# Moving the output projection one unit later, and part of a convolution from VectorE to ScalarE and GpSimd, in a two-layer attention kernel

## The chip, the core and the metric

The kernel runs on one NeuronCore of a Trainium2 chip. A core has five engines with a queue of instructions each: TensorE (PE; its weight loads are shown apart, as PEld), VectorE (DVE), ScalarE (ACT), GpSimd (POOL) and SyncE (SP), which here only issues DMAs. The engines meet at semaphores. The metric is the device time of one execution in microseconds (us); the profile comes from one execution of its own.

## The reference, cut to what matters

Two layers follow each other on an input of 8 images with 32 x 32 positions and 512 channels, all in float32. The first layer is group norm and self-attention (8 heads of 64 over all 1024 positions). The second layer is attention whose keys and values are sampled at learned places:

```python
x_ln = layernorm(x); q = x_ln @ wq + bq
o = depthwise_conv7x7_stride2(q, dw_w)           # 1024 positions -> 256, 49 taps a channel
o = gelu(o + dw_b)
offsets = conv1x1(o, pw_w)                       # 512 channels -> 2
grid = refs + tanh(offsets)                      # 256 places in the image
interp = bilinear_sample(x, grid)                # 4 rows of x weighted, for each place
k = v = interp @ wv + bv
attn = softmax((q @ mq_w) (k @ mk_w)^T); att = attn @ (v @ mv_w)     # 8 heads, 1024 x 256
z = att @ mo_w + mo_b + x
out = gelu(layernorm(z) @ mlp_w + mlp_b) + z
```

Everything is computed, and in float32. The convolution, the sampling and what depends on them are per image; one convolution chunk is 128 channels of one image (4 chunks an image).

## The kernel before, in words

The kernel has two passes, one for each layer, with tensors in DRAM between them (`mid` is the first layer's result, `hat_d` its normalised transpose). The first pass also computes the convolution of images 0 to 5 (`EARLY = 6`); there ScalarE multiplies a tap into a buffer (`part_x`) and GpSimd adds it to the sum (`oa`), while VectorE does other taps in one instruction each (`od`). The convolution of images 6 and 7 (8 chunks) is left to the second pass, which is what the change touches.

The second pass runs 64 **units**. A unit is one pair of heads (`hp`, 4 of them) of one half of an image (`hi`, 16 of them: 512 queries against 256 keys), `n = 4*hi + hp`. Nothing is scheduled by a planner: each step is entered with `at(place, step)`, a place is a unit's number plus a fraction, `run_due` sorts all steps by place, and a wrapper (`InOrder`) keeps every engine's instructions in that program order. So the fractions are the order in every queue, SP's and POOL's too, and an instruction that waits holds up all that stands behind it on its engine.

What a unit `n` does before the change, in order of place:

- `n`: `scores` (PE: `sc`; DVE: two row maxima `nmax`; ACT: 8 exponentials `e`).
- `n + 0.09`, `0.1`: `product` of the unit before (PE: `av`, needs `et`), `scale` (DVE: `attH`).
- `n + 0.11`, `0.13`: `moved` for each head (DVE: block transpose `sq`; SP: `sq` to DRAM as `sq_d`, and back, re-ordered, as `et`).
- `n + 0.12`: `joined`, the output projection of one tile of 128 rows, of the half image whose four units came before (PE: `wo`; DVE: `z` and its statistics; POOL: one power, `mv`, for the norm). The power is written by `rstd`.
- `n + 0.17`: `query_step` for the next unit (PE: `hat_h`; ACT: `q`).
- `n + 0.26` to `0.93`: nine convolution taps on DVE (`chunk`), with `norm` (DVE: `zn`) at `0.47`, `fill` of the next convolution chunk (PE: `wq_r`; DVE: `pad`) at about `0.5`, `share` (DVE: `rep`) at `0.54`.
- `n + 0.6`, `0.62`, `0.72`: `turned` (PE transposes `zn`; ACT: `zT`), `turn` (PE transposes `rep`; ACT: `inv`), `mlp` (PE: `wm`).
- `n + 0.95` to `0.97`: `biased` (DVE: `res`), and for every second tile the GELU of two tiles (ACT, with a table load each way), and `end` (POOL: `res + z` and the DMA out, twice).

Rows of `x` for the residual (`xr`) are fetched for two tiles at once at `pair - 0.7` (SP) and get their bias at `pair - 0.5` (POOL), where `pair` is the first of the two tiles' places. Once an image, at places counted from `last = 8*b - 4`: `conv_gelu`, `offsets`, `targets` (17 small DVE instructions), two times `gather` (POOL: 4 indirect DMAs, `row`) and `sample` (DVE: 4 instructions, `smp`); then four `key_step` and two `value_step` on PE. The PSUM pool for projections has three buffers (`mm`), used in turn.

The queue order of the four places that matter for what follows can be read in `back_steps` (`places`), `unit_steps`, `conv_steps` and `point_steps`:

Of the kernel before, what the change touches and what calls it, by code (L numbers as in the profile page):

```python
# [17 lines left out]
P = 128  # L18
# [213 lines left out]
def attention_then_deformable_attention(  # L232
# [115 lines left out]
    def at(place, step):  # L348
        due.append((place, len(due), step))
# [452 lines left out]
    with ExitStack() as l1:  # L802
# [52 lines left out]
        pads = [cv.tile([P, PADH, PADW], F32, tag=f"pad{i}", name=f"pad{i}") for i in range(PADS)]  # L855
        for pad in pads:
            nc.gpsimd.memset(pad, 0.0)
        att = Attention(nc, ident, ps_mm, ps_sc, ps_av, work, dram)
        smps = {}

# [52 lines left out]
            hat = chat[b, cb]  # L913
            room["ps"] = project(lambda c: hat[:, par * NC + c, :], lambda c: wq_r[:, c, :])

        def fill_end(cb, par):
            conv_pad(pads[cb % PADS], room["ps"], bq_row, par)

        def tap(b, cb, i):
            if i == 0:  # L920
                room["chunk"] = cv.tile([P, NS], F32, tag="chunk", name="chunk", bufs=2)
            conv_tap(room["chunk"], pads[cb % PADS], dww, cb, i, i == 0)
            if i == KS * KS - 1:
                nc.gpsimd.dma_start(o_d[b][:, cb, :], room["chunk"])

        def conv_gelu(b):
            o = room[b, "o"]
# [3 lines left out]
        def offsets(b):  # L931
            o = room[b, "o"]
            ps = mm_tile()
            for h in range(2):
                for cb in range(NC):
                    nc.tensor.matmul(
                        ps[:, ts(h, 2)], lhsT=o[:, cb, ts(h, P)], rhs=pww[:, cb, :],
                        start=(cb == 0), stop=(cb == NC - 1),
                    )
            room["th"] = cv.tile([P, 4], F32, tag="th", name="th")  # L940
            nc.scalar.activation(room["th"], ps[:, 0:4], AF.Tanh)

        def targets(b):
            room[b, "ii"], room[b, "wt"] = corners(room["th"])
# [110 lines left out]
        def back_steps(hi, start, step, tail=False):  # L1055

            b, half = divmod(hi, 2)
            xs = mid[b].rearrange("(t p e) c -> e t p c", e=2, p=P)[half]
            outs = out_tok[b].rearrange("(t p e) c -> e t p c", e=2, p=P)[half]
            xr, z, zn, zT, res = {}, {}, {}, {}, {}  # L1060

            def fetch(t):
                xr[t] = tmp("xr", 4)
                nc.sync.dma_start(xr[t], xs[t])

            def add(t):
                nc.gpsimd.tensor_tensor(xr[t], xr[t], bo_row, ALU.add)

            def joined(t):
                ps = project(lambda c: attH[hi][:, c, ts(t, P)], lambda c: wo[:, c, :])  # L1070
                z[t] = tmp("z", 5)
                nc.vector.tensor_tensor(z[t], ps, xr[t], ALU.add)
                stats = work.tile([P, 6], F32, tag="stats", name="stats")
                mv = xr["mv", t] = work.tile([P, 3], F32, tag="mv", name="mv")
                nc.vector.bn_stats(stats, z[t])
                nc.vector.bn_aggr(mv[:, 0:2], stats)
                rstd(mv[:, 2:3], mv[:, 1:2], 1e-5)

            def norm(t):
                zn[t], mv = tmp("zn", 2), xr["mv", t]  # L1080
                nc.vector.tensor_scalar(
                    zn[t], z[t], mv[:, 0:1], mv[:, 2:3], ALU.subtract, ALU.mult
                )

            def turned(t):
                ps = mm_tile()
                for c in range(NC):
                    nc.tensor.transpose(ps[:, ts(c, P)], zn[t][:, ts(c, P)], ident)
                zT[t] = tmp("zT", 2)
                nc.scalar.copy(zT[t], ps)  # L1090

            def mlp(t):
                res["ps", t] = project(lambda c: zT[t][:, ts(c, P)], lambda c: wm[:, c, :])

            def biased(t):
                res[t] = tmp("res", 3)
                nc.vector.tensor_tensor(res[t], res["ps", t], bm_row, ALU.add)

            def gelu(t):
                nc.scalar.activation(res[t], res[t], AF.Gelu)  # L1100

            def end(t):
                nc.gpsimd.tensor_tensor(res[t], res[t], z[t], ALU.add)
                nc.gpsimd.dma_start(outs[t], res[t])

            for t in range(NC):
                n, pair = start + step * t, start + step * (t - t % 2)
                places = (pair - 0.7, pair - 0.5), (n + 0.12, n + 0.47), (n + 0.6, n + 0.72, n + 0.95)
                if tail:
                    places = (n - 0.7, n - 0.6), (n, n + 0.01), (n + 0.11, n + 0.12, n + 0.125)  # L1110
                steps = (fetch, add), (joined, norm), (turned, mlp, biased)
                for place, what in zip(sum(places, ()), sum(steps, ())):
                    at(place, lambda t=t, what=what: what(t))


                if t % 2 == 1:
                    for what, after in ((gelu, 0.96), (end, 0.97)):
                        for i in (t - 1, t):
                            at(n + (0.13 if tail else after), lambda i=i, what=what: what(i))

        def unit_steps(n):
            hi, hp = divmod(n, NHP)
            b = hi // 2
            u = dict(tiles=NQT, at=0, v=lambda j, h: vals[b][:, j, ds((2 * hp + h) * HD, HD)])

            def scores():
                u["q"], u["k"] = queries.pop((hi, hp)), keys[b][:, hp, :]
                u["e"] = att.scores(u)  # L1130

            def scale():
                if hp == 0:
                    attH[hi] = work.tile([P, NHP, QB], F32, tag="attH", name="attH")
                att.scale(attH[hi][:, hp, :])

            at(n, scores)
            at(n + 0.11, lambda: att.moved(u, 0))
            at(n + 0.13, lambda: att.moved(u, 1))
            at(n + 0.54, lambda: att.share(u["sums"]))  # L1140
            at(n + 0.62, att.turn)
            at(n + 1.09, lambda: att.product(u))
            at(n + 1.1, scale)
            if n + 1 < 2 * B * NHP:
                at(n + 0.17, lambda: query_step(*divmod(n + 1, NHP)))


        def conv_counts():
            taps = (B - EARLY) * NC * KS * KS
            return [0, 0] + [9] * (taps // 9) + [taps % 9]  # L1150

        def conv_places():

            places = []
            for n, count in enumerate(conv_counts()):
                for j in range(count):
                    x = j / count
                    x = 0.26 + 0.2 * x / 0.45 if x < 0.45 else 0.57 + 0.36 * (x - 0.45) / 0.55
                    places.append(n + x)
            taps = KS * KS  # L1160
            return [places[i : i + taps] for i in range(0, len(places), taps)]

        def conv_steps():
            chunks, filled = conv_places(), -2
            for k, places in enumerate(chunks):
                b, cb = EARLY + k // NC, k % NC
                free = max(filled, chunks[k - PADS][-1] if k >= PADS else filled)
                slots = [n + 0.49 for n in range(60) if free < n + 0.49 < places[0] - 0.05]
                slots = (slots[:2] if k < PADS else slots[-2:]) if len(slots) > 1 else [slots[0], slots[0] + 0.26]
                filled = slots[1]  # L1170
                at(slots[0] - 1.8, lambda b=b, cb=cb: conv_fetch(b, cb))
                for par, place in enumerate(slots):
                    at(place, lambda b=b, cb=cb, par=par: fill(b, cb, par))
                    at(place + 0.04, lambda cb=cb, par=par: fill_end(cb, par))
                for i, place in enumerate(places):
                    at(place, lambda b=b, cb=cb, i=i: tap(b, cb, i))

        def point_steps(b):
            last = 2 * NHP * b - NHP
# [1 line left out]
            at(last - 0.035, lambda: conv_gelu(b))  # L1181
            at(last + 0.535, lambda: offsets(b))
            at(last + 0.75, lambda: targets(b))
            for h, (p0, p1) in enumerate(((0.8, 1.3), (1.31, 1.7))):
                at(last + p0, lambda h=h: gather(b, h))
                at(last + p1, lambda h=h: sample(b, h))

            first = 2 * NHP * b
            for hp, place in enumerate((-1.82, -1.81, 0.48, 2.18)):
                at(max(first + place, last + 2.18), lambda hp=hp: key_step(b, hp))  # L1190
            for t, place in enumerate((-0.82, 0.11)):
                at(first + place, lambda t=t: value_step(b, t))

        def load_late():
# [32 lines left out]
        for hi in range(2 * B):  # L1227
            if hi > 1:
                at(NHP * (hi - 1) - 1, lambda hi=hi: fetch_hat(hi))
            if hi + 1 < 2 * B:  # L1230
                back_steps(hi, NHP * (hi + 1), 1)
            else:
                back_steps(hi, NHP * (hi + 1) + 0.2, 0.1, tail=True)
        run_due(float("inf"))


# [31 lines left out]
```

## Time and profile before

| | before |
|---|---|
| median of 3 runs | 3657.85 us (3655.79 to 3663.18) |
| the profiled execution | 3652.66 us, of which the span from the first to the last instruction is 3650.9 us |
| first pass and preparation of the second | 0 to 2307.8 us |
| units 0 to 62 of the second pass | 2307.8 to 3580.7 us |
| unit 63 and the end | 3580.7 to 3650.9 us |

A unit's start is the start of its first `sc` matmul. All instructions carry line 54, that of the wrapper, so groups are told apart by the tiles that they write and read. "Idle before" in a timeline is the time for which the engine stood still before the instruction, and behind the arrow stands what ended it. Busy times are recorded for a matmul from its start to a modelled end, so neighbours overlap by about 0.1 us. A matmul in float32 is recorded twice (4 matmuls are x8).

### The profile page before, as it was taken

The page shows a single profiled execution, that of the slowest core. Times are in us where ns is not written, and L with a number is a line of the kernel's source. Part 1 is how long each engine was busy: PE and PEld are TensorE (multiplying, and loading weights), DVE is VectorE, ACT ScalarE, POOL GpSimd, SP SyncE. Part 2 cuts the span into 40 slices and gives each one's busy share as a digit, 9 for nine tenths or more (in the row PEclk, how much of TensorE's full clock was granted, in tenths as well). Part 3 has the DMA queues.
Part 4 walks back from the last instruction along what each step waited for, and adds up shares of the span by engine and source line. Part 5 has one row for each costly group of instructions (what it writes and reads, how often), then busy time and mean ns, then how long its engine had stood idle before and what let it go on. Part 6 is the DMA issues. An engine that isn't in the chain of part 4 may idle for free. (4 is left out here: it accounts for less than half of the span.)

```text
span 3650.9 us, 45574 instructions
## 1 busy us (share of the span) xinstructions
PE 3477.3 (95%) x15128; PEld 1743.3 (48%) x15128; DVE 2585.2 (71%) x3614; ACT 1763.8 (48%) x3740; POOL 1382.4 (38%) x1667
## 2 busy tenths in 40 slices
PE   7999999999999999999999989889999998989997
PEld 4554554554554554554554544444444444444443
DVE  4767688888888888888887873376766766674553
ACT  3443365575575575575575541234333433344442
POOL 1002236646646646646646634022222222221312
PEclk9999999999999999999999999999999999999999
DMA  4656657657657657657656665344444444354442
GB/s 143 162 153 174 179 151 209 173 152 207 174 153 206 176 151 202 180 151 199 182 147 193 193 168 175 117 164 155 168 159 145 167 146 174 129 180 167 173 143 100
DMA packets 358268, 606.00 MB, mean 166 GB/s; under 512 B 54577, under 2 KB 152881, under 8 KB 355985
## 3 DMA queue, kind: packets, MB, share of 16 engines
q1 hardware_dynamic: 327072, 499.94, 46.0%
q0 software_dynamic: 29808, 101.05, 8.9%
q8 instruction: 121, 1.98, 0.2%
q10 hardware_dynamic: 1152, 2.10, 0.2%
q14 instruction: 115, 0.93, 0.1%
HBM read 212.83 MB, written 121.63 MB: 92 GB/s over the span
## 5 line engine op out<-in xcount | busy, mean ns | idle before, releaser
L54 ACT ACTIVATE e<-sc,nmax 128x1024 f32<-128x1024 f32 (+1 forms) x1024 | 803.7, 798 | 665.4 <-DVE nmax L54 664.8
L54 DVE TENSOR_REDUCE nmax<-sc 128x1 f32<-128x1024 f32 (+1 forms) x640 | 752.2, 1216 | 328.3 <-PE sc L54 327.3
L54 DVE STREAM_TRANSPOSE sq<-e 128x1024 f32<-128x1024 f32 x640 | 767.0, 1229 | 167.0 <-ACT e L54 148.8
L54 POOL TENSOR_TENSOR oa<-part_x,oa 128x256 f32<-128x256 f32 x852 | 646.7, 759 | 589.1 <-ACT part_x L54 543.4
L54 PE MATMUL sc<-k,q 64*128 64x512 f32 x2048 | 535.2, 619 | 15.4 <-ACT e L54 13.5
L54 ACT ACTIVATE part_x<-pad_x,dww_x 128x256 f32<-128x256 f32 x852 | 437.3, 543 | 231.4 <-POOL oa L54 228.9
L54 PE MATMUL av<-et,v 128*64 128x256 f32 x4096 | 501.3, 387 | 8.5 <-DMA et<-sq 7.9
L54 PE MATMUL mm<-xT,wqkv 128*128 128x512 f32 x1024 | 470.1, 603 | 3.1 <-issue 3.1
L54 PEld LDWEIGHTS av<-et,v 128*64 128x64 f32 x4096 | 274.1, 137 | 313.3 <-issue 162.1
L54 POOL TENSOR_TENSOR mv<-mv,minus_half 128x1 f32<-128x1 f32 x128 | 79.5, 621 | 764.7 <-DVE mv L54 758.2
L54 PEld LDWEIGHTS sc<-k,q 64*128 64x128 f32 x2048 | 185.8, 186 | 276.5 <-issue 193.3
L54 PEld LDWEIGHTS mm<-xT,wqkv 128*128 128x128 f32 x1024 | 187.6, 191 | 234.9 <-issue 229.2
L54 PE MATMUL mm<-wm,zT 128*128 128x512 f32 x512 | 265.2, 666 | 8.2 <-ACT zT L54 6.2
L54 PEld LDWEIGHTS mm<-wqkv,xT 128*128 128x128 f32 x2048 | 234.2, 192 | 20.4 <-issue 18.9
L54 PE MATMUL mm<-wqkv,xT 128*128 128x128 f32 x2048 | 243.4, 277 | 0.0
L54 PE MATMUL mm<-wo,attH 128*128 128x512 f32 x512 | 235.6, 603 | 0.0
L54 PE MATMUL mm<-w,attT 128*128 128x512 f32 x512 | 234.0, 602 | 0.0
L54 PE MATMUL mm<-hat_h,wqq 128*128 128x512 f32 x512 | 230.6, 593 | 0.0
L54 DVE SCALAR_TENSOR_TENSOR od<-pad_x,dww_x,od 128x256 f32<-128x256 f32 x276 | 218.4, 791 | 5.5
L54 ACT ACTIVATION_READ_ACCUMULATOR e<-sc,nmax 128x1 f32 x1024 | 209.1, 204 | 0.0
L54 POOL TENSOR_TENSOR xr<-xr,bo_row 128x512 f32<-128x512 f32 x64 | 82.1, 1301 | 332.4 <-DMA xr<-mid 229.7
L54 DVE SCALAR_TENSOR_TENSOR chunk<-pad,dww,chunk 128x256 f32<-128x256 f32 x384 | 190.9, 497 | 9.9
(159 smaller groups left out, 3621.5 us busy)
## 6 DMA issues: line engine op xcount, KB each, us to landing
et<-sq SPq DMA_DIRECT2D x2048, 128.0 KB, 2.7
sq_d<-sq SPq DMA_DIRECT2D x128, 512.0 KB, 2.8
et<-sq_d SPq DMA_DIRECT2D x128, 512.0 KB, 3.9
hat_h<-hat_d SPq DMA_DIRECT2D x16, 1024.0 KB, 7.1
xr<-mid SPq DMA_DIRECT2D x64, 256.0 KB, 4.3
out_dram<-res POOLq DMA_DIRECT2D x64, 256.0 KB, 2.3
x<-in_x_dram POOLq DMA_DIRECT2D x60, 256.0 KB, 3.9
w<-in_L_conv_w_out_dram POOLq DMA_DIRECT2D x14, 1024.0 KB, 7.7
```

What stands on the lines that cost most here:

```text
L54: return self.tc.keep_in_program_order(op(*args, **kwargs))
```

## The change

All edits are in the second pass.

1. `joined` moves from `n + 0.12` to `n + 0.05`, ahead of `product` (from `n + 0.09` to `n + 0.15`), and the whole back end of a half image (`back_steps`) starts one unit later, `NHP * (hi + 1) + 1`. `norm` moves from `n + 0.47` to `n + 0.13`, between the two `moved`. `share` moves from `0.54` to `0.2`. `end` and its pair of `fetch` and `add` keep their fractions, so they shift by one unit, from odd to even units.
2. The eight convolution chunks go into two lanes. Lane 0 (chunks 0, 3, 6) stays on DVE with 5 taps a unit, 3 in some units. Lane 1 (chunks 1, 2, 4, 5, 7) goes to ScalarE and GpSimd, 7 taps a unit at `n + 0.156`, with a new buffer `parts` for two products. Both `fill`s of a chunk stand in one unit. `conv_counts` and `conv_places` go away.
3. `sample` moves ahead of the taps (`last + 1.22` and `last + 2.22`), keys and values to other places; `offsets` computes its two rows as `[2, 256]` (4 matmuls), takes tanh, and turns it with two transposes.
4. At the end of the kernel (`tail`), `product` of the last unit stands behind the last regular tile, the steps of the last four tiles are ordered anew, each tile ends by itself, the last addition is on VectorE and the last DMAs out are on SP. `z` has 4 buffers in place of 5.

```diff
-        def tap(b, cb, i):
+        def tap(b, cb, i, lane):
             if i == 0:
-                room["chunk"] = cv.tile([P, NS], F32, tag="chunk", name="chunk", bufs=2)
-            conv_tap(room["chunk"], pads[cb % PADS], dww, cb, i, i == 0)
+                room["chunk", lane] = cv.tile([P, NS], F32, tag="chunk", name="chunk", bufs=PADS)
+            chunk = room["chunk", lane]
+            part = parts[:, i % 2, :] if lane else None
+            conv_tap(chunk, pads[lane], dww, cb, i, i == 0, part)
...
-            for h in range(2):
-                for cb in range(NC):
-                    nc.tensor.matmul(
-                        ps[:, ts(h, 2)], lhsT=o[:, cb, ts(h, P)], rhs=pww[:, cb, :],
+            for cb in range(NC):
+                nc.tensor.matmul(
+                    ps[0:2, 0:NS], lhsT=pww[:, cb, :], rhs=o[:, cb, :],
...
+                nc.tensor.transpose(room["th"][:, ts(h, 2)], th[:, ts(h, P)], ident[0:2, 0:2])
...
-                z[t] = tmp("z", 5)
+                z[t] = tmp("z", 4)
...
-                nc.gpsimd.tensor_tensor(res[t], res[t], z[t], ALU.add)
-                nc.gpsimd.dma_start(outs[t], res[t])
+                (nc.vector if tail else nc.gpsimd).tensor_tensor(res[t], res[t], z[t], ALU.add)
+                (nc.sync if tail else nc.gpsimd).dma_start(outs[t], res[t])
...
-                places = (pair - 0.7, pair - 0.5), (n + 0.12, n + 0.47), (n + 0.6, n + 0.72, n + 0.95)
+                places = (pair - 0.7, pair - 0.5), (n + 0.05, n + 0.13), (n + 0.6, n + 0.72, n + 0.95)
                 if tail:
-                    places = (n - 0.7, n - 0.6), (n, n + 0.01), (n + 0.11, n + 0.12, n + 0.125)
+                    turn = n + 0.15 + 0.005 * (t > 0)
+                    places = (n - 0.7, n - 0.6), (n, n + 0.01), (turn, n + 0.25, n + 0.26)
...
-            at(n + 0.11, lambda: att.moved(u, 0))
-            at(n + 0.13, lambda: att.moved(u, 1))
-            at(n + 0.54, lambda: att.share(u["sums"]))
+            at(n + 0.12, lambda: att.moved(u, 0))
+            at(n + 0.14, lambda: att.moved(u, 1))
+            at(n + 0.2, lambda: att.share(u["sums"]))
...
-            at(n + 1.09, lambda: att.product(u))
-            at(n + 1.1, scale)
+            at(n + (1.9 if last else 1.15), lambda: att.product(u))
+            at(n + (1.905 if last else 1.155), scale)
...
+            for lane, chunks in enumerate(((0, 3, 6), (1, 2, 4, 5, 7))):
+                free = 0.5 + lane
+                for k in chunks:
...
+                    fills = [first + 0.49, first + 0.55]
...
+                        points = unit % (2 * NHP) in range(NHP, NHP + 3)
+                        count = 7 if lane else 3 if points else 5
...
+                            place = 0.156 + 0.002 * j if lane else 0.25 + 0.01 * j
+                            at(unit + place, lambda b=b, cb=cb, i=i, lane=lane: tap(b, cb, i, lane))
...
-            for h, (p0, p1) in enumerate(((0.8, 1.3), (1.31, 1.7))):
+            for h, (p0, p1) in enumerate(((0.8, 1.22), (1.23, 2.22))):
...
-            for hp, place in enumerate((-1.82, -1.81, 0.48, 2.18)):
-                at(max(first + place, last + 2.18), lambda hp=hp: key_step(b, hp))
-            for t, place in enumerate((-0.82, 0.11)):
+            for hp, place in enumerate((-0.82, -0.815, 0.185, 1.18)):
+                at(first + place, lambda hp=hp: key_step(b, hp))
+            for t, place in enumerate((-0.81, 0.18)):
...
-                back_steps(hi, NHP * (hi + 1), 1)
+                back_steps(hi, NHP * (hi + 1) + 1, 1)
             else:
-                back_steps(hi, NHP * (hi + 1) + 0.2, 0.1, tail=True)
+                back_steps(hi, NHP * (hi + 1) + 1, 0.1, tail=True)
```

`conv_tap` itself was there before, and with a `part` it issues one multiplication on ScalarE and one addition on GpSimd (the first tap of a chunk writes the sum directly).

More of the change, by code (lines that the diff above doesn't have):

```diff
@@ L857, in attention_then_deformable_attention @@
             nc.gpsimd.memset(pad, 0.0)
+        parts = cv.tile([P, 2, NS], F32, tag="parts", name="parts")
         att = Attention(nc, ident, ps_mm, ps_sc, ps_av, work, dram)
@@ L914, in fill, with fill_end @@
             room["ps"] = project(lambda c: hat[:, par * NC + c, :], lambda c: wq_r[:, c, :])
-        def fill_end(cb, par):
-            conv_pad(pads[cb % PADS], room["ps"], bq_row, par)
-        def tap(b, cb, i):
+        def fill_end(lane, par):
+            conv_pad(pads[lane], room["ps"], bq_row, par)
+        def tap(b, cb, i, lane):
             if i == 0:
-                room["chunk"] = cv.tile([P, NS], F32, tag="chunk", name="chunk", bufs=2)
-            conv_tap(room["chunk"], pads[cb % PADS], dww, cb, i, i == 0)
+                room["chunk", lane] = cv.tile([P, NS], F32, tag="chunk", name="chunk", bufs=PADS)
+            chunk = room["chunk", lane]
+            part = parts[:, i % 2, :] if lane else None
+            conv_tap(chunk, pads[lane], dww, cb, i, i == 0, part)
             if i == KS * KS - 1:
-                nc.gpsimd.dma_start(o_d[b][:, cb, :], room["chunk"])
+                nc.gpsimd.dma_start(o_d[b][:, cb, :], chunk)
         def conv_gelu(b):
@@ L933, in offsets @@
             ps = mm_tile()
-            for h in range(2):
-                for cb in range(NC):
-                    nc.tensor.matmul(
-                        ps[:, ts(h, 2)], lhsT=o[:, cb, ts(h, P)], rhs=pww[:, cb, :],
[L938 to L941, printed above, removed]
+            for cb in range(NC):
+                nc.tensor.matmul(
+                    ps[0:2, 0:NS], lhsT=pww[:, cb, :], rhs=o[:, cb, :],
+                    start=(cb == 0), stop=(cb == NC - 1),
+                )
+            th = cv.tile([2, NS], F32, tag="th", name="th")
+            nc.scalar.activation(th, ps[0:2, 0:NS], AF.Tanh)
+            room["th"] = mm_tile()[:, 0:4]
+            for h in range(2):
+                nc.tensor.transpose(room["th"][:, ts(h, 2)], th[:, ts(h, P)], ident[0:2, 0:2])
         def targets(b):
@@ L1113, in back_steps @@
                     at(place, lambda t=t, what=what: what(t))
[L1116 to L1119, printed above, removed]
+                ends = [t - 1, t] if t % 2 and not tail else [t] if tail else []
+                for what, after in ((gelu, 0.96), (end, 0.97)):
+                    for i in ends:
+                        at(n + (after - 0.69 if tail else after), lambda i=i, what=what: what(i))
         def unit_steps(n):
@@ L1137, in unit_steps @@
             at(n, scores)
-            at(n + 0.11, lambda: att.moved(u, 0))
-            at(n + 0.13, lambda: att.moved(u, 1))
-            at(n + 0.54, lambda: att.share(u["sums"]))
+            at(n + 0.12, lambda: att.moved(u, 0))
+            at(n + 0.14, lambda: att.moved(u, 1))
+            at(n + 0.2, lambda: att.share(u["sums"]))
             at(n + 0.62, att.turn)
-            at(n + 1.09, lambda: att.product(u))
-            at(n + 1.1, scale)
-            if n + 1 < 2 * B * NHP:
+            last = n + 1 == 2 * B * NHP
@@ L1145, in unit_steps @@
+            at(n + (1.9 if last else 1.15), lambda: att.product(u))
+            at(n + (1.905 if last else 1.155), scale)
+            if not last:
                 at(n + 0.17, lambda: query_step(*divmod(n + 1, NHP)))
[L1148 to L1161, printed above, removed]
@@ L1163, in conv_steps @@
-        def conv_steps():
[L1164 to L1176, printed above, removed]
+        def conv_steps():
+            for lane, chunks in enumerate(((0, 3, 6), (1, 2, 4, 5, 7))):
+                free = 0.5 + lane
+                for k in chunks:
+                    b, cb = EARLY + k // NC, k % NC
+                    first = next(n for n in range(60) if n + 0.49 > free)
+                    fills = [first + 0.49, first + 0.55]
+                    at(fills[0] - 1.8, lambda b=b, cb=cb: conv_fetch(b, cb))
+                    for par, place in enumerate(fills):
+                        at(place, lambda b=b, cb=cb, par=par: fill(b, cb, par))
+                        at(place + 0.02, lambda lane=lane, par=par: fill_end(lane, par))
+                    unit = int(fills[1]) + 1
+                    i = 0
+                    while i < KS * KS:
+                        points = unit % (2 * NHP) in range(NHP, NHP + 3)
+                        count = 7 if lane else 3 if points else 5
+                        for j in range(count):
+                            if i == KS * KS:
+                                break
+                            place = 0.156 + 0.002 * j if lane else 0.25 + 0.01 * j
+                            at(unit + place, lambda b=b, cb=cb, i=i, lane=lane: tap(b, cb, i, lane))
+                            free = unit + place
+                            i += 1
+                        unit += 1
```

## The prediction

> **What bounds the kernel now.** Only the second pass is edited, so I cut it into stretches with the table of busy times by stretch: units 0 to 4, 5 to 37, 38 to 62, and unit 63 with the end. Columns: length, then busy time of PE, PEld, DVE, ACT, POOL, then the granted PE clock.
>
> ```profile
> 2307.80:2404.50 96.70, 78.23 (x258) 35.53 (x258) 52.50 (x100) 31.34 (x99) 4.19 (x5) 0.93 0.38 136
> 2404.50:3103.10 698.60, 638.63 (x2186) 309.63 (x2185) 475.35 (x860) 266.24 (x737) 165.56 (x176) 0.96 0.45 160
> 3103.10:3580.70 477.60, 454.63 (x1595) 218.98 (x1594) 276.41 (x460) 199.17 (x553) 112.89 (x120) 0.99 0.44 159
> 3580.70:3651.00 70.30, 50.36 (x137) 22.08 (x136) 22.82 (x39) 12.13 (x29) 18.69 (x21) 0.88 0.21 75
> ```
>
> PE has 91% of the large stretch, at a clock of 0.96. The list of waits for 2320 to 3600 us says what it waits for, and where POOL stands:
>
> ```profile
> PE mm L54 <- DVE zn L54: 59.8, 27, 5.3
> POOL xr L54 <- DMA xr<-mid: 221.3, 31, 10.4
> ```
>
> The timeline of PE shows such a wait (unit 29) beside a unit without one (unit 49, 15.98 us long, the floor of a unit with nothing extra):
>
> ```profile
> 2922.42 1.12 PE L54 MATMUL mm<-ident,zn 128*128 128x128 f32 x4 [4.94 <-DVE zn L54]
> 2923.33 1.06 PE L54 MATMUL mm<-ident,rep 128*128 128x128 f32 x4
> 2924.21 5.30 PE L54 MATMUL mm<-wm,zT 128*128 128x512 f32 x8
> ...
> 3339.41 0.66 PE L54 MATMUL mm<-ident,zn 128*128 128x128 f32 x4
> 3340.75 3.70 PE L54 MATMUL mm<-wm,zT 128*128 128x512 f32 x8
> ```
>
> A wait of 5 us costs twice: the `wm` behind it takes 5.30 us in place of 3.70. So `zn` stands too late behind DVE's taps and samples, and this is what the change removes. But `zn` has a second parent, POOL's power `mv`. SP in unit 49 (start 3328.40), then POOL in unit 50 (start 3344.38):
>
> ```profile
> 3334.98 0.32 SPq L54 DMA_DIRECT2D sq_d<-sq  x1
> 3337.64 0.37 SPq L54 DMA_DIRECT2D et<-sq_d  x1
> 3338.95 0.32 SPq L54 DMA_DIRECT2D sq_d<-sq  x1
> 3342.79 0.37 SPq L54 DMA_DIRECT2D et<-sq_d  x1
> 3343.21 0.97 SPq L54 DMA_DIRECT2D xr<-mid  x2
> ...
> 3347.74 2.50 POOL L54 TENSOR_TENSOR xr<-xr,bo_row 128x512 f32<-128x512 f32 x2 [9.36 <-DMA xr<-mid]
> 3350.19 1.28 POOL L54 TENSOR_TENSOR res<-res,z 128x512 f32<-128x512 f32 x1
> 3352.37 1.28 POOL L54 TENSOR_TENSOR res<-res,z 128x512 f32<-128x512 f32 x1
> 3354.65 0.56 POOL L54 TENSOR_TENSOR mv<-mv,minus_half 128x1 f32<-128x1 f32 x1
> ```
>
> The `xr` DMAs are queued behind both heads' `sq_d` and `et`, POOL stands 9.36 us for them, and only after two additions and two `end`s comes the power: 6.9 us from 3347.74 to 3354.65. It starts 10.3 us into unit 50, and `zn` (3355.65) just makes it for PE.
>
> **What the Trainium skill says.** "TensorE: Matmul & The Clock Gate", Part 1, halves PE's clock after an idle window of about 3.4 us; the 5.30 against 3.70 above agrees in kind. The same page's table of specs has VectorE, ScalarE and GpSimd strictly first in, first out; the lines above agree. "GPSIMD Engine Reference", Key points, has GpSimd share its SBUF interfaces with VectorE, for instructions with two SBUF inputs or two ports; here a tap on DVE takes 791 ns beside POOL's additions in the first pass (`od`), 497 in the second (`chunk`).
>
> **The change part by part.** I walk one unit with durations of the timeline; zero is its first `sc`.
>
> *Even unit, no taps.* PE: `sc` to 1.9, `wo` to 5.6, `av` to 7.4, `hat_h` to 10.9. DVE: `z` at 5.65, statistics to 7.4 (1.75 after `z`, as in unit 43), first `sq` 7.4 to 8.6, `zn` to 9.1 (power at 7.55 to 8.1), second `sq` to 10.25, `attH` to 10.9, `rep` at 11.5. PE turns `zn` at 10.9, `rep` at 11.55, and `wm` runs from 12.2 (`zT`) to 15.9. No wait: the floor.
>
> *Its xr.* `sq` now starts at 7.4, where unit 49 had 5.3. `sq_d` issues at 8.7, `et` 2.7 later at 11.35, second `sq_d` at 11.75, its `et` 5.2 later (unit 50: 3355.92 to 3361.09) at 16.9, `xr` at 17.35, POOL's addition 4.5 later (3343.21 to 3347.74) at 21.9. The order is unchanged, the whole is 2.5 us later than unit 49's 19.3.
>
> *Odd unit, no taps.* POOL reaches the power at 21.9 + 6.9 - T, T being the even unit's length; for T = 15.9 that is 12.9. The old place of `zn` behind both `sq` hid such a delay; now second `sq`, `attH` and `rep` are queued behind the waiting `zn`: `zn` 13.5 to 14.0, `sq` to 15.2, `attH` to 15.8, `rep` to 16.35, PE's `rep` to 16.9, `wm` to 20.5. PE idles 5 us between 10.9 and 16.9, so `wm` is slow, 1.7 us more: 22.2. The pair takes 38.1; before, units 59 and 60 took 33.3, and 61 and 62 34.2.
>
> *Taps on ACT and POOL.* The first pass shows the pace: POOL did six `oa` in 5.13 us (0.855 each), some stretches 0.78; I take 0.82. With two slots in `parts`, ACT's tap 6 starts when POOL's fifth addition ends. Even unit: exponentials end at 7.2, power ends 8.1, additions from 8.2, tap 6 ends 12.85, `q` to 13.4, `zT` to 14.0, `wm` to 17.7. PE idles 2.3 of 3.2 us; of seven such waits (2.6 to 2.8 us) before, four slowed `wm`, so I add 0.6: 18.3. Odd unit: the exponentials start 1.3 later (ACT_TABLE_LOAD, 1283 ns), and the additions stand behind the power, at 28.8 - 18.3 = 10.5. From there: power 0.6, five additions 4.1, tap 0.55, `q` 0.6, `zT` 0.6, `wm` 3.65, slow 1.7: 22.3. Pair: 40.6; before, 9 taps on DVE: units 18 and 19 36.8, 26 and 27 38.5.
>
> *Points.* `gather` now shares its parity with `xr` and `end`: four rows at 1.33 us (1.03 and a gap of 0.3), 5.3 us more ahead of the power. Unit 8b - 4 has `offsets` on PE (4 matmuls like a key step's, 1.85; before 1.84), then PE waits for tanh behind ACT's taps: 21. The odd unit: power at 28.8 + 5.3 - 21 = 13.1, end at 24.7. Pair 45.7 (before 43.7 to 46.3); unit 13 with two fills and samples ahead of `pad` on DVE 27.5.
>
> *Sums.* Units 0 to 4 have no tile to project, and the first no fill: 20.8, 14.8, 16.9 (waiting for `et`), 13.1, 15.8 = 81.4, -15. Units 5 to 37: four plain pairs 162; four point pairs 3 x 45.7 + 48.5 = 186; unit 5, with gather and `xr` of a short unit 4, 25; the sixteen units around new keys 16 x 16.0, four sets of keys and values at 14.3 (4 x 1.85 + 2 x 3.45), five pairs of fills at 6.9, and 13 for waits on ACT = 361. In all 734, +35 (7 of it fills that stood in 38 and 39). Units 38 to 62: four plain pairs 152.4 and one even unit; two point pairs, 43.6 each; twelve units around keys 235 = 490, +12. The end: one tile more (7.5), unit 63 an odd one (+6), ends on DVE and SP and the new order -6: +8. `offsets(0)` in preparation waits for tanh: +1. Fewer `z` buffers cost nothing while POOL frees them within two units; lost cover would cost the wait for an `end`, 1.3.
>
> -15 + 35 + 12 + 8 + 1 = +41. The profiled execution, 3652.7 with what lies around its span, would take 3694; the median stood 5.2 above it: 3699, **I say 3698 us**.
>
> Unknown, bounded: DVE beside POOL, from no slowing to twice (1.3 us a tap unit, 43 in all, if `rep` then holds `wm`); the slow clock, from none (-37: 22 odd units at 1.7) to all counted.
>
> **Rivals.** (1) *No slow clock*: same waits, `wm` at 3.7: 3698 - 37 = 3661, no change. Against it: five waits of 4.9 us or more all slowed `wm`. (2) *Faster*: POOL's block ends before the power is needed, and the gain is what the words promise. Place: start of odd units; price: plain pairs 31.9 and 36.4, about 60 under before in all with -15 at the start, -20 and -26 in the two stretches, +1: 3598. It decides where `xr` lands early enough for the power to start by about 9 us; for that `xr` would have to be issued 3 to 4 us sooner than SP's order gives. For it: DVE loses 245 of its 392 taps, and `zn` no longer stands behind any. (3) *Worse*: DVE is slowed by POOL to twice: 3698 + 43 = 3741; `od` had single ones of 1.9 us. (4) The change doesn't do what it says, as `zn` waits for POOL where it waited for DVE: that is the forecast.
>
> **How the numbers follow.** Forecast 0.50 (own range 3675 to 3725), no slow clock 0.12, faster 0.25, worse 0.13. Within 0.2% (7 us, about what runs of 3656 to 3663 can tell) lies half of the second: 0.06; a quarter of it on each side: faster 0.28, slower 0.66. The range, 3605 to 3730, leaves out about half of (2) and half of (3).
>
> **What would show it.** Right: in odd units POOL's `xr`, `res`, `mv` in this order, `mv` at 10 to 13 us; PE waiting for `zn` and then `rep`, longest in plain units after 40; clock below 0.96 in 38 to 62; even plain units at 16 without taps, 18 with. Wrong, if `mv` starts before 9 us in odd units, if odd plain units late in the pass take under 18 us, or if units 5 to 37 take under 690 us.

## The result, and the profile after

The changed kernel takes 3708.49 us (median of 4 runs, 3702.22 to 3709.46), the kernel before beside it 3657.2 (4 runs, 3655.79 to 3663.18): 1.0133 times as long, with an interval of 1.0116 to 1.0151. It is slower by 51 us. The profiled execution took 3709.09 us with a span of 3707.4.

First the table of busy times by stretch of the kernel after, cut at the same units as before (0 to 4, 5 to 37, 38 to 62, 63 with the end). Columns: length, busy time of PE, PEld, DVE, ACT, POOL, granted PE clock, share and rate of the DMAs.

```profile
2310.97:2393.50 82.53, 66.85 (x232) 30.53 (x232) 44.94 (x62) 36.90 (x111) 9.97 (x13) 0.96 0.42 146
2393.50:3137.50 744.00, 657.25 (x2179) 306.98 (x2178) 441.43 (x718) 385.35 (x975) 337.83 (x405) 0.94 0.43 150
3137.50:3631.70 494.20, 453.44 (x1565) 215.02 (x1564) 235.78 (x389) 203.27 (x557) 106.64 (x115) 0.96 0.44 154
3631.70:3707.40 75.70, 56.88 (x157) 25.40 (x156) 28.55 (x49) 14.52 (x32) 18.20 (x20) 0.90 0.24 85
```

The start won 14 us. The large stretch lost 45: its PE has 19 us more of busy time (638.6 to 657.3, at a clock of 0.94 in place of 0.96), and stands still for the other 27. Of the 19, 6 are fills that stood in units 38 and 39 before (`wq_r`: 36.0 to 42.2); the `wm` of this stretch take no more in all than before (141.8 for 142.4), as the kernel before had slow ones too. DVE has less to do in every stretch but the last, and it does not help. Stretch three has no convolution on ACT and POOL and no fills any more, and still lost 17 us.

The list of waits between 2320 and 3600 us (total, times, longest), the same window as for the kernel before:

```profile
POOL xr L54 <- DMA xr<-mid: 310.9, 38, 14.9
DVE zn L54 <- POOL mv L54: 96.2, 21, 9.5
PE mm L54 <- DVE zn L54: 57.2, 13, 8.1
PE mm L54 <- DVE rep L54: 22.5, 15, 2.5
PE mm L54 <- ACT zT L54: 27.8, 50, 1.6
```

PE's wait for `zn` has almost the total it had (57.2 for 59.8), but in half as many waits, each twice as long. Behind it stands a second link that was hardly there before: DVE itself waits 96 us for POOL's power `mv` (before, not once in this window). The wait for `rep` behind it grew from 15.9 to 22.5. ACT is late for PE as well: the waits for `zT` grew from 3.4 to 27.8, and five waits for `q`, 12.3 in all, are new. ACT's taps wait for POOL's additions to free one of the two product buffers (139.8 us), and `q` and `zT` stand behind them.

The timelines of POOL, then DVE, then PE in unit 59, an odd unit without taps (start 3556.10, length 21.96):

```profile
3562.07 2.51 POOL L54 TENSOR_TENSOR xr<-xr,bo_row 128x512 f32<-128x512 f32 x2 [13.86 <-DMA xr<-mid]
3564.53 1.27 POOL L54 TENSOR_TENSOR res<-res,z 128x512 f32<-128x512 f32 x1
...
3568.85 0.57 POOL L54 TENSOR_TENSOR mv<-mv,minus_half 128x1 f32<-128x1 f32 x1
...
3569.46 0.55 DVE L54 TENSOR_SCALAR zn<-z,mv 128x512 f32<-128x512 f32 x1 [3.08 <-POOL mv L54]
3569.92 1.24 DVE L54 STREAM_TRANSPOSE sq<-e 128x1024 f32<-128x1024 f32 x1
...
3571.87 0.43 DVE L54 COPY rep<-rs 128x512 f32<-128x512 f32 x1
...
3570.06 0.66 PE L54 MATMUL mm<-ident,zn 128*128 128x128 f32 x4 [2.83 <-DVE zn L54]
3572.35 1.05 PE L54 MATMUL mm<-ident,rep 128*128 128x128 f32 x4 [1.64 <-DVE rep L54]
3573.20 4.93 PE L54 MATMUL mm<-wm,zT 128*128 128x512 f32 x8
```

Read it from the top. POOL stands 13.86 us for rows that arrive 6 us into the unit, then works through two additions and two `end`s, and only then gives the 0.57 us power, 12.75 us into the unit. DVE had the statistics ready long before (its `mv` ended at 3565.20). Behind the late `zn` stand the second `sq`, `attH` and `rep`, so PE waits a second time, and the `wm` that follows runs 4.93 us for 3.70. Even units have none of this: unit 58 took 16.01 us.

### The profile page after: what moved, and what is told of

It is laid out like the page before. It is cut to its first block, busy times and chain, and to the rows that moved or that the text cites. A ratio compares the mean times of both kernels' runs of the same rounds, so it can differ in the third digit from the quotient of the medians.

```text
span 3707.4 us, 45821 instructions
## 1 busy us (share of the span) xinstructions
PE 3489.8 (94%) x15080; PEld 1734.0 (47%) x15080; DVE 2510.2 (68%) x3373; ACT 1894.5 (51%) x3997; POOL 1553.1 (42%) x1899
## 4 chain that ended last, share of the span: by engine, by line
PE 79%; POOL 6%; DMA 6%; ACT 3%; issue 3%; DVE 3%; SPq 1%; POOLq 0%; ACTq 0%; DVEq 0%
PE mm L54 50%; PE sc L54 15%; PE av L54 13%; DMA xr<-mid 2%; DMA sq_d<-sq 2%; POOL chunk L54 1%; ACT e L54 1%; POOL xr L54 1%; POOL res L54 1%; SPq L54 1%; DVE sq L54 1%; POOL row L54 1%; DVE nmax L54 1%; ACT zT L54 0%; DMA et<-sq 0%
## 5 line engine op out<-in xcount | busy, mean ns | idle before, releaser
L54 POOL TENSOR_TENSOR chunk<-parts,chunk 128x256 f32<-128x256 f32 x240 | 185.7, 774 | 114.7 <-ACT parts L54 98.5
L54 DVE TENSOR_TENSOR res<-mm,bm_row 128x512 f32<-128x512 f32 x64 | 44.3, 692 | 264.7 <-PE mm L54 261.3
```

What stands on the lines that cost most here:

```text
L54: return self.tc.keep_in_program_order(op(*args, **kwargs))
```

## The experiments

The stretches and the span are those of each kernel's own profiled execution, cut at the same units; the medians and ratios are over all of its runs. Each ratio is to runs of the kernel before that were taken beside it (their medians: 3657.2 for the changed kernel, 3654.2 for 1 to 4, 3657.9 for 5 to 8), so it isn't the quotient of two medians of the table. Times in us.

| kernel | units 0 to 4 | 5 to 37 | 38 to 62 | 63 and end | span | median | ratio to before |
|---|---|---|---|---|---|---|---|
| before | 96.6 | 698.6 | 477.6 | 70.2 | 3650.9 | 3657.2 | |
| after | 82.5 | 744.0 | 494.3 | 75.7 | 3707.4 | 3708.49 | 1.0133 (1.0116 to 1.0151) |
| 1: after, `xr` fetched earlier | 82.4 | 685.4 | 452.8 | 71.2 | 3604.4 | 3606.81 | 0.9875 (0.9855 to 0.9896) |
| 2: after, `end` behind the power | 84.2 | 771.3 | 466.5 | 74.6 | 3706.9 | 3705.15 | 1.0134 (1.0116 to 1.0151) |
| 3: after, `norm` behind `share` | 80.5 | 748.0 | 474.7 | 74.4 | 3683.1 | 3694.47 | 1.0114 (1.0091 to 1.0136) |
| 4: after, no ACT/POOL taps | 83.7 | 701.4 | 494.6 | 75.9 | 3665.7 | 3672.59 | 1.0053 (1.0034 to 1.0071) |
| 5: before, `norm` and `share` earlier | 94.2 | 668.8 | 478.3 | 68.7 | 3626.2 | 3619.83 | 0.9885 (0.9855 to 0.9916) |
| 6: after, `end` behind the taps | 82.3 | 693.1 | 469.2 | 73.1 | 3624.4 | 3631.54 | 0.9927 (0.9901 to 0.9952) |
| 7: before, `xr` fetched earlier | 99.0 | 706.5 | 485.3 | 69.8 | 3673.0 | 3673.23 | 1.0037 (1.0029 to 1.0046) |
| 8: after, 1 and 6 together | 80.5 | 672.8 | 452.1 | 71.2 | 3586.8 | 3588.1 | 0.981 (0.9782 to 0.9839) |

The theory: POOL's block, held by the `xr` DMAs that SP issues too late, delays the power in odd units, and with it all that stands behind `zn`. The rivals are named in each expectation.

### 1: the rows fetched one unit earlier

```diff
-                places = (pair - 0.7, pair - 0.5), (n + 0.05, n + 0.13), (n + 0.6, n + 0.72, n + 0.95)
+                places = (pair - 1.7, pair - 0.5), (n + 0.05, n + 0.13), (n + 0.6, n + 0.72, n + 0.95)
```

> The changed kernel with the residual rows xr fetched one unit earlier (pair - 1.7 in place of pair - 0.7); nothing else moves, only SP's queue and so the time at which POOL's additions can start. Theory (POOL's queue, held by the late xr, delays the power, and zn holds DVE): the additions then run in the even unit, the power starts 7.6 to 9 us into odd units, PE's waits for zn go, plain pairs take 32 us without taps and 36 to 37 with, units 38 to 62 take 450 to 458 us (494 now), units 5 to 37 680 to 700 (744 now): about 3605 us in all, 3590 to 3630. Rival 1 (ScalarE's and GpSimd's taps are what costs): units 38 to 62 fall, units 5 to 37 stay above 725, about 3655 to 3665. Rival 2 (the two end additions alone hold the power, or DVE is slowed by POOL): within 15 us of 3708.

Measured: 3606.81, 102 us under the changed kernel and 1.25% under the kernel before the change. The timelines of POOL in units 58 and 59 (starts 3452.82 and 3468.84), then of PE in unit 59:

```profile
3460.39 0.55 POOL L54 TENSOR_TENSOR mv<-mv,minus_half 128x1 f32<-128x1 f32 x1 [17.05 <-DVE mv L54]
3460.92 2.67 POOL L54 TENSOR_TENSOR xr<-xr,bo_row 128x512 f32<-128x512 f32 x2
...
3476.49 0.55 POOL L54 TENSOR_TENSOR mv<-mv,minus_half 128x1 f32<-128x1 f32 x1 [3.94 <-DVE mv L54]
...
3481.50 3.70 PE L54 MATMUL mm<-wm,zT 128*128 128x512 f32 x8 [0.38 <-ACT zT L54]
```

The additions to `xr` now stand in the even unit with no wait for a DMA, the odd unit's power waits only for its own parent on DVE and starts 7.65 us into the unit, PE waits nowhere for more than 0.4 us, and the unit takes 16.3 in place of 22.0. The same SP, the same DMAs, the same POOL work: the place of two DMAs in SP's queue is worth the whole loss and more. What is left are the odd units with both gathers and taps: their power starts at 9.6 to 12.2, and they take 22.0 to 24.8, where four gathers and two `end`s still stand ahead of it (experiment 8 moves the `end`s).

### 2: the two additions of `end` behind the power

```diff
-                        at(n + (after - 0.69 if tail else after), lambda i=i, what=what: what(i))
+                        at(n + (after - 0.69 if tail else 1.06 if what is end else after), lambda i=i, what=what: what(i))
```

> The changed kernel with the step end placed behind the power of the next unit (n + 1.06 in place of n + 0.97), still ahead of the taps. xr stays late. Theory: the power starts at 24.4 minus the even unit's length, 8.5 us without taps, so units 38 to 62 fall to 452 to 465 us; but with taps POOL's additions stand behind both ends, 4.4 us, so odd units with taps stay at 22 to 24 us and units 5 to 37 stay within 15 us of 744. In all about 3665 us. If the power alone mattered: units 5 to 37 fall to under 710, 3630 or less. If the xr wait weren't in the chain: no change.

Measured: 3705.15, no gain: the expected total was missed. The stretches show two things that cancel: units 38 to 62 won 28 us (466.5, within 2 us of what was expected), and units 5 to 37 lost 27, where within 15 was expected. The timelines of POOL, ACT and PE in unit 19 (start 2719.04, length 24.26):

```profile
2726.68 0.55 POOL L54 TENSOR_TENSOR mv<-mv,minus_half 128x1 f32<-128x1 f32 x1 [2.00 <-DVE mv L54]
...
2731.53 5.82 POOL L54 TENSOR_TENSOR chunk<-parts,chunk 128x256 f32<-128x256 f32 x7
...
2732.30 0.56 ACT L54 ACTIVATE parts<-pad,dww 128x256 f32<-128x256 f32 x1 [5.38 <-POOL chunk L54]
...
2737.43 5.94 PE L54 MATMUL mm<-wm,zT 128*128 128x512 f32 x8 [5.67 <-ACT zT L54]
```

The power is on time, and now the two `end`s stand between it and the seven `chunk` additions. ACT has two product buffers, so its taps end with POOL's, and ACT's `zT` stands behind its taps: PE's wait moved from `zn` to `zT` and is longer. It also reached odd units that had been free: unit 17 went from 17.7 to 22.9, since an `end` now always stands ahead of the taps. The rival that only the power's time matters is out. So is the one that forecast no change, though the total shows none: stretch three, which has no taps, follows the power (unit 59: power at 9.3 in place of 12.75, length 17.7 in place of 22.0).

### 3: `norm` behind `share`

```diff
-                places = (pair - 0.7, pair - 0.5), (n + 0.05, n + 0.13), (n + 0.6, n + 0.72, n + 0.95)
+                places = (pair - 0.7, pair - 0.5), (n + 0.05, n + 0.21), (n + 0.6, n + 0.72, n + 0.95)
```

> The changed kernel with norm at n + 0.21 in place of n + 0.13: zn still ahead of the taps on DVE, but behind the second sq, attH and rep, so these no longer wait for the power. Theory (the waiting zn holds second sq, attH and rep, about 2 us of the odd units' length): plain odd units without taps lose 1.5 to 2.5 us, with taps less than 1 as ScalarE sets wm there; in all 10 to 20 us faster than the changed kernel, about 3693. Rival (the delay of zn alone costs, the queue behind it is hidden): within 5 us of 3708.

Measured: 3694.47 (3684.81 to 3701.88; the profiled execution is the fastest of these). The timeline of PE in unit 59 (start 3539.39, length 18.37):

```profile
3552.80 0.66 PE L54 MATMUL mm<-ident,zn 128*128 128x128 f32 x4 [2.28 <-DVE zn L54]
3553.29 0.60 PE L54 MATMUL mm<-ident,rep 128*128 128x128 f32 x4
3554.13 3.70 PE L54 MATMUL mm<-wm,zT 128*128 128x512 f32 x8 [0.24 <-ACT zT L54]
```

The power is as late as before (12.2 us into the unit), but it holds only `zn`: `rep` is there, the second wait of 1.64 is gone, and behind one idle time of 2.28 us the `wm` takes 3.70 (not always: 5.40 behind 2.52 in unit 51). The unit is 3.6 us shorter and stretch three 19.6. So in these profiled executions about half of the 41.5 us that experiment 1 won in that stretch is won with a late power too, by what had been put behind `zn` on DVE. Where POOL and ACT have taps (units 5 to 37) it brings nothing: PE waits for `zT` there in place of `rep` (3.73 us in unit 19).

### 4: the taps of ACT and POOL left out

```diff
-            conv_tap(chunk, pads[lane], dww, cb, i, i == 0, part)
+            if not lane or i == 0:
+                conv_tap(chunk, pads[lane], dww, cb, i, i == 0, part)
```

> The changed kernel without the taps of lane 1 after each chunk's first (240 multiplications on ScalarE and 240 additions on GpSimd are left out, so five convolution chunks are not computed). Theory: odd units keep POOL's late power, so plain pairs in units 5 to 37 take about 38 us as later in the pass, and the stretch takes 690 to 710 us (744 now), units 38 to 62 stay at 494: about 3665 us. Rival 1 (the taps are the cause): the stretch falls to the floor of PE, about 650 us, and the total to 3615.

Measured: 3672.59. Units 5 to 37 take 701.4, 43 less, and units 38 to 62 are unchanged. The 240 taps on ACT and POOL so cost 43 us of span in their stretch, as long as the power is late. Even without them, and with over half of DVE's taps gone too, that stretch is no faster than before the change (698.6). The power of the odd units is as late as before (unit 11: at 13.4 us, length 22.5); that this alone took the gain is not shown apart.

### 5: in the kernel before, `norm` and `share` ahead of taps and samples

```diff
-                places = (pair - 0.7, pair - 0.5), (n + 0.12, n + 0.47), (n + 0.6, n + 0.72, n + 0.95)
+                places = (pair - 0.7, pair - 0.5), (n + 0.12, n + 0.2), (n + 0.6, n + 0.72, n + 0.95)
...
-            at(n + 0.54, lambda: att.share(u["sums"]))
+            at(n + 0.21, lambda: att.share(u["sums"]))
```

> The kernel before with two places changed: norm at n + 0.2 (was 0.47) and share at n + 0.21 (was 0.54), both behind the two sq and ahead of all taps; nothing else of the change. Theory: PE's waits for zn and rep go (80 us of the second pass stand before zn and rep, and about 16 slow wm of 1.7 us go with them), POOL's power at 9.4 to 10.3 is still in time as zn stands behind the second sq; about 3590 us, 3570 to 3615. Rival (the waits only move on, to the pads, samples and res behind the taps): 3640 or more.

Measured: 3619.83, 1.15% under the kernel before and 30 us above what was expected. From its list of waits between 2320 and 3600 us:

```profile
PE mm L54 <- DVE z L54: 22.4, 7, 4.2
...
PE mm L54 <- DVE zn L54: 3.0, 3, 2.5
```

The waits for `zn` are gone (3.0 for 59.8), and nine units that had waited 2.6 to 5.3 us for it are at the floor of 16.0. But PE now waits for `z` as long as 4.2 us at a time (before, 1.5 in all): in units 14, 22 and the like (every eighth from 6 to 54) the samples on DVE are late (in unit 22 they wait 1.8 and 3.1 us for gathered rows), `z` with them, and a `key_step` that stands behind on PE; unit 22 grew from 23.4 to 31.4, and these seven units together from 152.8 to 196.3. So the part of the change that takes `norm` out from behind the taps is sound; it needs neither another place for the projection nor other engines, and what is missing of the expected gain (30 of 67 us) is less than what these seven units lost.

### 6: `end` behind the taps of POOL

```diff
-                        at(n + (after - 0.69 if tail else after), lambda i=i, what=what: what(i))
+                        at(n + (after - 0.69 if tail else 1.2 if what is end else after), lambda i=i, what=what: what(i))
```

> The changed kernel with end at n + 1.2, behind the power and behind the taps of lane 1; xr stays late. Theory: with taps the power needs only xr and its two additions, 24.4 minus 17.5 is 6.9, so it starts at 7.6 as in even units and the odd plain units take 17.6; units 5 to 37 take 680 to 695 us (771 with end between power and taps, 744 in the changed kernel); without taps the power starts at about 9 and units 38 to 62 take 460 to 468 as with end between. In all about 3620 us. Rival (the late xr is what holds the queue, the ends don't matter): above 3690.

Measured: 3631.54, with 693.1 and 469.2 us in the two stretches: 78 us less than experiment 2 in the first, by a place behind seven additions in place of ahead of them. Unit 19 takes 17.6. This confirms the reading of 2. `xr` is as late as in the changed kernel: unit 43 still has its power at 10.0 and takes 18.4.

### 7: in the kernel before, the rows fetched one unit earlier

```diff
-                places = (pair - 0.7, pair - 0.5), (n + 0.12, n + 0.47), (n + 0.6, n + 0.72, n + 0.95)
+                places = (pair - 1.7, pair - 0.5), (n + 0.12, n + 0.47), (n + 0.6, n + 0.72, n + 0.95)
```

> The kernel before with xr fetched one unit earlier, the edit that tells in the changed kernel. Theory: there the power of even units starts at 9.6 to 10.3 and zn stands behind the second sq and five taps, so the same late xr was hidden: within 8 us of the kernel before. Rival (the late xr cost the kernel before too, so the edit is a gain of its own): 20 us or more faster.

Measured: 3673.23, slower by 0.37%, where no change was expected; the rival, 20 us faster, is out. The timelines in unit 43 (start 3226.14; before 3208.56) of POOL, DVE and PE:

```profile
3236.09 2.67 POOL L54 TENSOR_TENSOR xr<-xr,bo_row 128x512 f32<-128x512 f32 x2
...
3236.59 4.02 DVE L54 SCALAR_TENSOR_TENSOR chunk<-pad,dww,chunk 128x256 f32<-128x256 f32 x5
...
3241.12 1.11 PE L54 MATMUL mm<-ident,zn 128*128 128x128 f32 x4 [4.05 <-DVE zn L54]
...
3242.91 5.24 PE L54 MATMUL mm<-wm,zT 128*128 128x512 f32 x8
```

and the same taps and the same wait in the kernel before:

```profile
3219.02 2.52 DVE L54 SCALAR_TENSOR_TENSOR chunk<-pad,dww,chunk 128x256 f32<-128x256 f32 x5
...
3221.46 0.54 DVE L54 TENSOR_SCALAR zn<-z,mv 128x512 f32<-128x512 f32 x1
```

With the rows there early, POOL's two additions run beside DVE's five taps, which take 0.80 us each in place of 0.50. `zn` is 1.5 us later, PE's wait grows from 2.56 to 4.05, and the `wm` behind it from 3.70 to 5.24: 3.5 us for one unit. The six units with this wait (9, 19, 25, 35, 41 and 43) took 14.1 us more together; the others gain and lose. The late `xr` of the kernel before was harmless there, and even kept POOL out of DVE's way. The same edit makes the one kernel 2.7% faster and the other 0.4% slower.

### 8: both edits, 1 and 6, in the changed kernel

The diff is that of 1 and that of 6.

> The changed kernel with both moves, xr one unit earlier and end behind the taps. Theory: what is left in the first of them, odd point units (13, 21, 29, 37 and 5, at 22 to 25 us, power at 9.6 to 12.2 behind four gathered rows and two ends), loses 3 to 5 us each: units 5 to 37 665 to 672 us (685 with xr alone), the rest unchanged, about 3588 us in all. Rival (PE's floor and ScalarE's taps are all that is left): 3600 to 3607.

Measured: 3588.1, 1.9% under the kernel before and 3.2% under the changed one. The timeline of POOL in unit 21 (start 2716.85), an odd unit with gathers and taps:

```profile
2724.49 0.56 POOL L54 TENSOR_TENSOR mv<-mv,minus_half 128x1 f32<-128x1 f32 x1 [2.11 <-DVE mv L54]
2725.04 6.09 POOL L54 TENSOR_TENSOR chunk<-parts,chunk 128x256 f32<-128x256 f32 x7
2731.09 1.71 POOL L54 TENSOR_TENSOR res<-res,z 128x512 f32<-128x512 f32 x1
```

Power, taps and `end` stand in the order in which others need them, and the unit takes 17.6 us in place of 26.3. It is the fastest version of this study.

## Why the prediction was right, and where it was off

The forecast was 3698 with an own range of 3675 to 3725; the median is 3708.5. By its steps:

- **The chain, `xr`, additions, `end`s, `mv`, `zn`, then `rep`**: right, and shown by experiments 1 (cut at `xr`), 6 (cut at the `end`s) and 3 (cut behind `zn`). Unit 59 was to have its power at 12.9 and take 22.2; it has 12.75 and 21.96. Even units without taps take 16.0 (15.9). `sq_d` and `et` of the even unit came at the times given.
- **Units 0 to 4**: -15 predicted, -14.2 measured. **Preparation**: +1, measured +3.2, which is no more than the preparation differs between kernels whose preparation is the same (it ends at 2305.6 to 2312.6 in the changed kernel and its six variants). **The end**: +8, measured +5.5.
- **Units 5 to 37**: +35 predicted, +45.4 measured. The sixteen units around new keys, summed at 361, took 361.4, unit 5 26.1 (25), the four point pairs 189.5 (186), and the four plain pairs 167.0 (162), which is half of the miss. T, the even unit's length, was too long: even units with taps took 17.5 us, not 18.3, as no slow clock came after their wait of 1.6 us. But the power of the odd unit comes at 28.8 - T, so a shorter even unit makes the odd one wait longer by as much, and the sum of a pair doesn't depend on T. The term that was too small is `wm`: 5.9 to 6.1 us in units 11, 19 and 27 for 5.35. In unit 35 it took 6.25, and the rows of `xr` landed 6.2 and 6.3 us after their issue, so the power came at 13.2 where 28.8 - T gives 11.3. Point pairs show the trade between even and odd too: the wait for tanh was 0.7 us and the even units took 18.8 for 21, the odd ones 26.3 to 32.1 for 24.7 to 27.5.
- **Units 38 to 62**: +12 predicted, +16.7 measured, again in the plain pairs (157.4 for 152.4). Two of their odd units are longer than predicted, 43 (25.2) and 51 (24.6). Their power came at 15.2 and 14.1. I had taken one landing time for `xr` from unit 49; but right behind it SP issues the 512 KB of `o` and the 1024 KB of `hat_h`, and in unit 43 the two rows landed 5.0 and 7.0 us after their issue, for 4.2 and 3.9 in unit 59, where nothing stood behind. It is much the same over the changed kernel's second pass: the second row took 4.6 to 7.0 us with `o`, `hat` or `hat_h` behind it, and 3.9 to 4.7 without, but for 5.5 and 5.7 in units 32 and 45. The Trainium skill ("Trainium Kernel Development and Optimization", Key Constraints) says that DMAs issued from the SP, ACT and POOL queues all run on the same 16 DMA engines and interleave. It speaks of several queues; here all stand in SP's, the numbers would fit, and no run shows that the later transfers are the cause.
- **The sum**: the parts of the span came to +56.5 where I had +41. Some 5.8 of these 15.6 us came back in the median, since I had set it 5.2 above the profiled execution, as it stood before the change, and this time it lies 0.6 below. That the forecast is off by 10.5 us and not by 16 is luck.
- **The signs**: `xr`, `res`, `mv` stand in this order. Two signs were put too simply. PE's longest waits for `zn` are in the point units 29 and 45 (8.1 and 7.1), not in plain ones after 40. And the power starts before 9 us, which was to mean "wrong", in eight odd units (9, 17, 25, 31, 33, 41, 49 and 57; in the others it starts at 11.2 to 17.6, for the 10 to 13 forecast). There the even unit before takes 21 us or more, so POOL's block ends within it, and 28.8 - T gives 7.7 or less. Such units have nothing to win: seven of them take the same in experiment 1, and 33 takes 1.1 us less.
- **Rival 1, no slow clock**: out. `wm` takes 4.65 to 6.4 us in the odd units where PE waits for `zn`; in experiment 3 it is at 3.70 again in units 43, 59 and 61.
- **Rival 2, faster**: out for this kernel, right in its condition and nearly in its price. It was to decide where `xr` is issued early enough; experiment 1 did that, with 452.8 in units 38 to 62 for 451.6, and 3606.8 in all for 3598. The first of the two stretches fell short (685.4 for 678.6).
- **Rival 3, DVE slowed by POOL**: the mechanism is there, its price is not. DVE's taps in units 5 to 37 take 0.679 us for 0.493 before, `zn` in unit 19 0.95 for 0.55 in unit 59. `zn` and `rep` stand in PE's way, but in unit 19 ACT's `zT` came later still, and DVE's taps stand behind nearly all that PE needs. Only for a fill's `pad`, which stands behind taps and samples, did PE wait (2.80 us in unit 13, and 3.23 in unit 30 of experiment 8). In experiment 8 the taps take 0.955, and the stretch is the shortest of the changed kernel's versions.
- **In the expectations**: experiment 2's total and size were missed, since I had priced the `end`s ahead of the taps for the units where they were late already, not for those that had not waited for them (17, 31, 33). Experiment 5 left out what is late next, the samples. Experiment 7 left out what an earlier transfer sets going beside it.

Left open: unit 30 of experiment 8 still takes 27.6 us, where `pad` on DVE is late (PE waits 3.23 us for it).

## What to carry to other kernels

In queues that run strictly in order, ask of every small instruction that others wait for (here a power of 0.57 us) what stands ahead of it, and follow that to the DMA that it waits for: moving work to a less loaded engine, or moving a consumer closer to its producer, gains nothing where it lands behind such a wait. When a consumer is moved ahead of its old neighbours, all of these are behind it from then on, and a delay that had cover before reaches them too. And a fetch can be as harmful early as late: look at what it sets going, and beside whom.

## What the runs showed of the hardware

- The slowing of DVE by POOL depends on the instruction. Beside POOL's `xr` additions, five taps took 4.02 us for 2.52 (experiment 7), and `zn` 1.06 for 0.51 (unit 58 of experiment 1, and of the changed kernel). The block transpose `sq` that ran beside the same addition kept its time (1.23 for 1.24). "GPSIMD Engine Reference", Key points, names instructions with two SBUF inputs or in a mode with two ports; the taps, with two SBUF inputs, agree with it, `zn` has one tensor input, and would by that page have to be in such a mode, which no run here shows.
- How long `wm` takes behind a wait doesn't follow from the length of the wait alone. Behind one idle time of 2.56 or 2.57 us it took 3.70 in units 19, 41 and 43 of the kernel before, and 5.24 to 5.40 in its units 9, 25 and 35. Behind some 1.55 us, in experiment 8, it took 3.70 in unit 19 and 5.40 in units 11, 35 and 37 (granted clock during it: 1.00 in unit 19, 0.68 in unit 11). Behind one idle time of 4.05 us or more, of which units 4 to 62 of the ten kernels have 49, it took 4.4 us at the least. So the idle window of about 3.4 us that the prediction names isn't a limit below which `wm` keeps its 3.70. Whether two waits with short transposes between them count as one is open: behind 2.83 and 1.64 us `wm` took 4.93 (the changed kernel), behind 0.99 and 1.64 it took 3.60 in unit 43 of experiment 6, and behind 0.84 and 1.64 it took 4.90 in its unit 59.
